# GpSimd ropes q in the second part of a linear attention kernel; one k is summed in PSUM

## The chip, the cores and the metric

The kernel runs on one core of a Trainium2 chip. The metric is the device time of the core in microseconds (us). The core's engines run side by side, each through its own queue in order, and wait for each other on semaphores: TensorE (PE in the profile; PEld is its loading of weights), VectorE (DVE), ScalarE (ACT), GpSimd (POOL) and SyncE (SP), which issues most DMAs. TensorE writes into PSUM, of which there are 8 banks of 128x512 float32 numbers; DVE and ACT read and write PSUM and SBUF; POOL reads and writes SBUF alone.

## The reference

For x of 16 x 1024 rows of 512 numbers:

```python
qkv = x @ Wqkv.T + bqkv
q, k, v = jnp.split(qkv, 3, axis=-1)
q = rmsnorm(q, gq); k = rmsnorm(k, gk)
# 16 heads of 32 numbers
q = apply_rope(q, cos, sin); k = apply_rope(k, cos, sin)
qf = relu(q); kf = relu(k)
vk = einsum('bhlp,bhld->bhpd', [v, 1], kf)
res = einsum('bhpd,bhld->bhlp', vk, qf)
attn = res[..., :-1] / (res[..., -1:] + EPS_LIN)
out = rmsnorm(attn @ Wout.T + bout, gout)
x = layernorm(x + out)
# then a feed-forward layer on x mixed with the row before it
r = sigmoid(xr @ W_r.T); k = square(relu(xk @ W_k.T))
x = layernorm(x + r * (k @ W_v.T))
```

The rope turns pairs of numbers: out_r = t_r cos - t_i sin, out_i = t_r sin + t_i cos. vk is a sum over all 1024 rows of a batch, so q of a batch can be used only when all its k are done.

## The kernel before

Every product in float32 is made of three products of a high and a low half: x = xh + xl and w = wh + wl give xh wh + xh wl + xl wh. ACT makes the high half by a copy that rounds, DVE or POOL the low half by a subtraction. A tile is 128 rows of x; there are 128 tiles, 8 in a batch.

**First part.** It computes q and k of each tile from x's transposed tiles (xt), ropes both, stores q to DRAM (q_d), and adds k into the state of its batch (pskx, four banks; the products of L584, 12 for each tile). The first 8 tiles (SOLO) are done one by one. The other 120 are done as 60 pairs of tiles a and b (`pair`, L1034), which share block products in the manner of Strassen and Winograd: seven products p1 to p7 of six matmuls each (`block_product`, L993) instead of the eight that q and k of two tiles would need. Sums and differences of quarters of xt (s1 to s4, `block_sum`) are made by POOL; their halves, and those of the quarters a1, a2 and a4, by ACT (high, L988) and POOL (low, L990), in `split_block_steps`.

Within a pair, p7 goes to a bank z, which ACT copies into an SBUF tile k2 (`z_out`, L1073). p1 and p2 go to the bank of q of tile a, which ACT has filled with the bias beforehand (`seed`, for the next pair at L1134); between p1 and p2 ACT copies this bank into that of q of b (`y_seed`, L1077). p6 is added to the latter; then DVE writes k of a as this sum and the bias (L1081), adds k2 (L1082), p5 goes to k of a, DVE adds k of a to k2 (`k2_add`, L1085), p4 completes q of b, and p3, in the next pair, k of a. The second half of b_qk holds k's bias less q's (L1270), since the seed carries q's. The next pair begins with p7, then the last pair's p3, then p1, the rest of the last pair's state products, and p2. At the end of a batch the state is turned into m_d, a matrix with the output projection in it (`finish_a`, `finish_b`, `finish_c`).

The rope (`rope_in_steps`, L506) is one squaring on ACT, whose sum goes to rmsnorm, and three operations on DVE: two multiplications by tables (L516 and L518, whose first operand is PSUM except for k of b, which lies in SBUF as k2) and an addition with swapped halves (L521). Its two tables of 256 KB for each q or k are loaded from DRAM by SP (L432), in a ring of five tiles. `rope_k_steps` then makes the reciprocal root on POOL (L148), the halves of relu(k) on ACT (L541, L545) and DVE (L548); POOL adds k to the batch's sum of keys (L556). `split_xn_steps` makes the halves of x for the state (L376 on ACT, L378 on DVE).

From the 29th pair on (WOVEN), output products of the first tiles are interleaved with the pairs.

The order of work around the change is written out by hand as due times: `at(t, fn)` and `steps_at` note that a step is due at t, in units U of one matmul, and all steps are issued in the order of their due times (L1287). PE keeps this order. A scheduler places the instructions of the other engines in their queues by its own model of time.

**Second part** (from L1449, loop at L1533). For each tile j: q of tile j+2 is loaded (`load_q`, L216; three buffers in all), `part_q` (L242) multiplies q of tile j+1 by the sum of keys and scales it on DVE (L246 to L254), `part_qt` transposes it on PE and splits it, `part_m` multiplies it by m_d (psy), `part_y` adds it to x and normalizes (L318, POOL's L148, L327). Between these stand the products of the feed-forward layer (`part_t`, `part_fk`, `part_fr`, `part_fv`) for groups of four tiles. POOL's work here is one low half a tile (mkl, L1335) and the reciprocal roots of L148.

Of the kernel before, what the change touches and what calls it, by code (L numbers as in the profile page):

```python
# [15 lines left out]
P = 128  # L16
# [6 lines left out]
NQ = 1  # L23
# [11 lines left out]
def kernel(  # L35
# [169 lines left out]
    def load_ks(b):  # L205
        ksb[b] = ring("ks", b + (b > 0), 1, 1, [P, DIM], F32, f"ksb{b}")
# [22 lines left out]
    def load_x(j, src=None, early=False):  # L229
        if early:  # L230
            xs[j] = tp.tile([P, DIM], F32, tag="xw", bufs=2, name=f"xw{j}")
        else:
            xs[j] = x_tile(j)
        nc.sync.dma_start(out=xs[j], in_=x[j] if src is None else src)

    def heads(tl):
# [95 lines left out]
    with ExitStack() as a_ctx:  # L332
# [563 lines left out]
        def early(i):  # L896
# [5 lines left out]
            else:  # L902
                tables()
            if i > 1:
                seed(i + 1, 0)
# [46 lines left out]


        def quads():
            for i in range(SOLO, N, 2):
                yield from ((i, 0), (i + 1, 1), (i + 1, 0), (i, 1))

# [22 lines left out]
        def split_block_steps(i, n):  # L980
# [8 lines left out]
            yield  # L989
            G.tensor_sub(t[:, 1], src, f32(t[:, 0]))  # L990

# [42 lines left out]
        def pair(i, t):  # L1034
# [17 lines left out]
            def p1():  # L1052
                block_product(first[a, 0], blk("a1"), lambda w, c: w_q[w][:, c, :])

            def p2():
                block_product(first[a, 0], blk("a2"), lambda w, c: w_q[w][:, 2 + c, :])

# [13 lines left out]
            def z_out():  # L1071
                me["k2"] = rope_tile(b, 1)
                S.copy(me["k2"], me["z"])  # L1073

            def y_seed():
                me["y"] = bank(f"psq{b}")
                S.copy(me["y"], first[a, 0])  # L1077

# [5 lines left out]
            def k2_add():  # L1084
                V.tensor_add(me["k2"], me["k2"], me["a"])  # L1085

            def rope_q_a():
                yield from rope_in_steps(a, 0, first.pop((a, 0)))
                tables()
                load_xn(b)  # L1090

            def rope_k_b():
                yield from rope_in_steps(b, 1, me["k2"], me["k2"])
                tables()

            def rope_q_b():
                yield from rope_in_steps(b, 0, me["y"])
                tables()

            def rope_k_a():  # L1100
                yield from rope_in_steps(a, 1, me["a"])
                tables()

# [27 lines left out]
            tq = tx2 if was is None else max(tx2, t0 + 12 * U + 3.1)  # L1131
            steps_at(rope_q_a(), t + 0.05, tq + 0.45, tq + 1.05, tq + 1.8)
# [6 lines left out]
            steps_at(xn_b, t + 0.45, t + 2.8)  # L1139
            at(t + 2.85, load_xn, a)  # L1140

# [68 lines left out]
            at(t, k2_add)  # L1210
            steps_at(rope_k_b(), t + 0.75, t + 0.8, t + 1.5, t + 2.2)
            at(t, p4)
            t += 6 * U
            steps_at(rope_q_b(), t + 0.05, t + 1.6, t + 2.2, t + 2.95)
            kb = later(rope_k_steps, b)
            steps_at(kb, t + 0.9, t + 1.0, t + 3.2, t + 6.5)
            at(t + 5.2, add_keys, b)
            ts = t + 12 * U
            steps_at(rope_k_a(), ts + 0.05, ts + 1.2, ts + 1.8, ts + 2.5)
            ka = later(rope_k_steps, a)  # L1220
            steps_at(ka, ts + 1.1, ts + 1.15, ts + 4.8, ts + 6.4)
            at(ts + 7.0, add_keys, a)
            xn_a = later(split_xn_steps, a)
            steps_at(xn_a, ts + 2.8, ts + 3.2)
            if r == 2 and j is not None:
                steps_at(later(part_q_steps, j), ty2 + 1.9, ts + 5.9)
            me["p3"], me["rest"] = p3, kx_rest
# [204 lines left out]
        wb = ctx.enter_context(tc.tile_pool(name="workb", reuse_waits="tile", bufs=1))  # L1432
        own["ks"] = wb
        part_fk(0, 0, ps=psk[0])
# [67 lines left out]
    def part_fv(s, t):  # L1502
# [15 lines left out]
        nc.sync.dma_start(out=out[j], in_=xs[j])  # L1518

    ffn = (  # L1520
# [12 lines left out]
    for s in range(NH):  # L1533
        order = ffn if s > 0 else ffn_first
        for u in range(NT):
            j = NT * (s + 2) + u
            if NPRE + NQ < j + 2 < N:
                load_q(j + 2)
            if NPRE + 1 <= j + 1 < N:
                load_x(j + 1)  # L1540
# [10 lines left out]
            if j < N:  # L1551
# [85 lines left out]
```

## Time and profile before

| what | value |
|---|---|
| median of 3 runs | 2866.84 us (2862.26 to 2874.19) |
| the profiled execution | 2863.01 us |
| its span, first to last instruction | 2861.2 us |
| first pair starts / last pair starts (L1073) | 94.6 us / 1320.7 us |
| table loads of 256 KB (L432) | 480, 3.9 us each from issue to landing |
| loads of q (L216) | 128, 2.7 us each |
| largest part of the chain that ended last | PE, 53% of the span |

The profile is that of one execution. Its page gives each engine's busy time, the span in 40 slices, the chain of waits that ended last, and the costliest groups of instructions by line with the mean time of one. Queries of its trace give the same for a stretch of time, the waits, and the timeline. A busy engine is not yet the bound; what counts in a stretch is which engine the others wait for there.

### The profile page before, as it was taken

To read this page: it belongs to the slowest core of one execution; us is meant where nothing else is said; L and a number is where in the kernel's file an instruction comes from. 1 tells how busy PE (TensorE), PEld (TensorE's weight loads), DVE (VectorE), ACT (ScalarE), POOL (GpSimd) and SP (SyncE) were. 2 spreads that over 40 slices of the span, in tenths; PEclk is the share of its full clock that TensorE was granted. 3 is DMA by queue.
4 is the path that set the end of the run, shared out by engine and by line. 5 is a ranking of instruction groups with operands and counts; after the bars stand their busy time and mean duration, and the time that the engine had idled before them with its cause. 6 is when DMAs were issued, how large, how long until landed. Compare 5 with 4: busy or idle time off the path is not lost.

```text
span 2861.2 us, 40565 instructions
## 1 busy us (share of the span) xinstructions
PE 2681.5 (94%) x12212; PEld 2171.1 (76%) x12212; DVE 2420.0 (85%) x4953; ACT 1936.5 (68%) x4068; POOL 1274.5 (45%) x1468
## 2 busy tenths in 40 slices
PE   8888888888988988988999999999999999999999
PEld 6666666666767776766788888888888888888887
DVE  9798788889999999997788888888888887888784
ACT  6556555556565656665687777777777777777876
POOL 6766666667676666674432222222222222222221
PEclk9999999999999999999999999999999999999999
DMA  7676666677877777778333132313232323232211
GB/s 234 199 228 221 213 214 204 206 230 243 260 247 246 232 243 236 236 237 285 122 104 114 56 111 85 115 58 109 88 112 61 106 92 108 65 102 93 91 46 41
DMA packets 240932, 450.08 MB, mean 157 GB/s; under 512 B 25268, under 2 KB 25780, under 8 KB 240712
## 3 DMA queue, kind: packets, MB, share of 16 engines
q1 hardware_dynamic: 240276, 446.83, 48.6%
q8 instruction: 96, 1.57, 0.2%
q14 instruction: 124, 1.02, 0.1%
q10 hardware_dynamic: 436, 0.66, 0.1%
HBM read 329.92 MB, written 117.47 MB: 156 GB/s over the span
## 4 chain that ended last, share of the span: by engine, by line
PE 53%; DVE 1%; DMA 0%; issue 0%; ACT 0%; POOL 0%; POOLq 0%; SPq 0%; DVEq 0%; ACTq 0%
PE psr L188 12%; PE psk L188 12%; PE psv L188 12%; PE psy L188 11%; PE pst L173 2%; PE psqt L173 2%; PE pskx L584 1%; PE psq L997 0%; DMA x<-x_d 0%; DMA w_k<-w_dk 0%; PE psk L997 0%; PE pskv L651 0%; DVE pr L246 0%; DVE t L516 0%; PE psm L700 0%
## 5 line engine op out<-in xcount | busy, mean ns | idle before, releaser
L188 PE MATMUL psk<-mkh,w_k 128*128 128x512 f32 x1024 | 331.9, 395 | 0.1
L188 PE MATMUL psv<-w_v,kah 128*128 128x512 f32 (+1 forms) x1032 | 322.3, 394 | 1.1 <-DVE gate L1514 1.1
L188 PE MATMUL psr<-w_r,mrh 128*128 128x512 f32 x1024 | 318.6, 396 | 0.6 <-DVE halo L1338 0.6
L990 POOL TENSOR_TENSOR blks<-parts,blks 128x256 fp32r<-128x256 f32 x240 | 209.7, 874 | 217.0 <-ACT blks L988 215.6
L188 PE MATMUL psy<-mb,qth 128*128 128x512 f32 x896 | 280.0, 389 | 0.0
L1335 POOL TENSOR_TENSOR mkl<-mixk,mkh 128x512 fp32r<-128x512 f32 x127 | 165.1, 1300 | 194.4 <-ACT mkh L1333 193.4
L556 POOL TENSOR_TENSOR acc<-acc,ro 128x512 f32<-128x512 f32 x112 | 167.2, 1493 | 152.5 <-ACT ro L545 148.9
L997 PE MATMUL psq<-wq_h,blka 128*128 128x512 f32 x480 | 179.8, 415 | 56.7 <-ACT psq L1077 56.7
L188 PEld LDWEIGHTS psk<-mkh,w_k 128*128 128x128 f32 x1024 | 191.3, 188 | 39.0 <-PE pst L173 0.3
L148 POOL TENSOR_TENSOR yrs<-yss,mhalf 128x1 f32<-128x1 f32 x128 | 70.7, 552 | 331.6 <-DVE yss L322 230.7
L188 PEld LDWEIGHTS psv<-w_v,kah 128*128 128x128 f32 x1032 | 188.8, 188 | 38.1 <-DVE gate L1514 1.5
L188 PEld LDWEIGHTS psr<-w_r,mrh 128*128 128x128 f32 x1024 | 188.7, 188 | 37.9 <-ACT r L1376 1.0
L148 POOL TENSOR_TENSOR rsa<-sqa,mhalf 128x1 f32<-128x1 f32 x128 | 79.6, 622 | 304.7 <-DVE sqa L304 293.8
L541 ACT ACTIVATE kh<-ro,rstd_all 128x512 fp32r<-128x512 f32 x128 | 92.7, 725 | 163.0 <-DVE ro L521 110.0
L188 PE MATMUL psv<-w_v,kal 128*128 128x512 f32 (+1 forms) x516 | 200.8, 389 | 0.0
L188 PE MATMUL psk<-mkl,w_k 128*128 128x512 f32 x512 | 199.8, 391 | 0.0
L188 PE MATMUL psr<-w_r,mrl 128*128 128x512 f32 x512 | 196.7, 394 | 0.0
L188 PEld LDWEIGHTS psy<-mb,qth 128*128 128x128 f32 x896 | 168.0, 188 | 34.8
L148 POOL TENSOR_TENSOR rsf<-sqf,mhalf 128x1 f32<-128x1 f32 x128 | 70.2, 555 | 265.6 <-DVE sqf L304 240.4
L584 PE MATMUL pskx<-kl,xnh 128*128 128x512 f32 x512 | 149.7, 400 | 32.7 <-DVE kl L548 32.7
L188 PE MATMUL psy<-mb,qtl 128*128 128x512 f32 x448 | 174.8, 390 | 0.0
L988 ACT CAST blks<-parts 128x256 fp32r<-128x256 f32 x240 | 97.7, 407 | 108.1 <-PE psk L997 67.3
(292 smaller groups left out, 8353.0 us busy)
## 6 DMA issues: line engine op xcount, KB each, us to landing
tab<-tab_d SPq DMA_DIRECT2D x480, 256.0 KB, 3.9
xt<-in_xt_dram SPq DMA_DIRECT2D x128, 256.0 KB, 4.0
xn<-in_x_dram SPq DMA_DIRECT2D x128, 256.0 KB, 3.5
q_d<-ro SPq DMA_DIRECT2D x128, 256.0 KB, 4.0
q<-q_d SPq DMA_DIRECT2D x128, 256.0 KB, 2.7
m_d<-m SPq DMA_DIRECT2D x64, 512.0 KB, 4.3
out_dram<-x SPq DMA_DIRECT2D x127, 256.0 KB, 2.0
x<-in_x_dram SPq DMA_DIRECT2D x120, 256.0 KB, 2.8
```

Of the source, the lines that this page charges most:

```text
L148: G.tensor_tensor(dst, src, mhalf[:, 0 : src.shape[1]], ALU.pow)
L173: T.matmul(ps[:, n * P : (n + 1) * P], lhsT=b, rhs=ident, is_transpose=True, start=(n == 0), stop=(n == NC_ - 1), skip_group_check=True,)
L188: T.matmul(ps, lhsT=a[u][:, rows], rhs=b[w][:, cols], start=(afresh and c == 0 and k == 0), stop=(c == n - 1 and k == 2), skip_group_check ...
L541: S.activation(kh, r, AF.Relu, scale=rstd_all[:, i, 1:2])
L556: G.tensor_add(acc[b], acc[b], r)
L584: T.matmul(ps_kx[b][c], lhsT=a[:, c * P : (c + 1) * P], rhs=r, start=(t == 1 and n == 0), stop=(t == 8 and n == 2),)
L988: S.copy(t[:, 0], src)
L990: G.tensor_sub(t[:, 1], src, f32(t[:, 0]))
L997: T.matmul(ps, lhsT=blk[:, u, c, :], rhs=rhs(w, c), start=(afresh and n == 0), stop=(n == len(order) - 1), skip_group_check=True,)
L1335: (V if by_v else G).tensor_sub(ml, m, f32(mh))
```

## The change

- q of the tiles from 10 on is no longer roped in the first part. DVE adds the bias to it on the way from PSUM to SBUF, ACT squares the result, and it is stored to q_d unroped (`q_out_steps`). In the second part its two tables are loaded (`load_tab`, L1534 of the changed kernel) and POOL ropes it in three operations (`rope_q`, L1539 to L1541), one tile ahead of its use by `part_q`.
- k of tile b is summed into a PSUM bank (`k2_add`), and its rope reads PSUM.
- The banks of q of a are no longer seeded with the bias; p1 starts its bank afresh. b_qk holds the plain bias of k.
- p1 stands ahead of the last pair's p3, `y_seed` after it, then p3, the rest of the state's products, and p2.
- The low halves of a1, a2 and a4 are made by DVE, those of s1 to s4 by POOL as before.
- Due times around these steps are written anew; the ring of tables has four tiles; the sum of keys ksb has one buffer of its own.

```diff
+    def late_q(j):
+        return j >= SOLO + 2
...
-                    tb = wa.tile([P, DIM], F32, tag="tab", bufs=5, name=f"tab{j}{n}{i}")
+                    tb = wa.tile([P, DIM], F32, tag="tab", bufs=4, name=f"tab{j}{n}{i}")
...
+        def q_out_steps(i, ps):
+
+            b_q = b_qk[:, 0:DIM]
+            if not late_q(i):
+                V.tensor_add(ps, ps, b_q)
+                yield
+                yield from rope_in_steps(i, 0, ps)
+                tables()
+                return
+            r = rope_tile(i, 0)
+            V.tensor_add(r, ps, b_q)
+            yield
...
+            S.activation(junk(f"{i}0"), r, AF.Square, accum_out=sums[i][:, 0:1])
+            q_d[i] = dram.tile([P, DIM], F32, name=f"q_d{i}")
+            nc.sync.dma_start(out=q_d[i], in_=r)
...
-            G.tensor_sub(t[:, 1], src, f32(t[:, 0]))
+            (G if n[0] == "s" else V).tensor_sub(t[:, 1], src, f32(t[:, 0]))
...
             def p1():
-                block_product(first[a, 0], blk("a1"), lambda w, c: w_q[w][:, c, :])
+                me["x"] = bank(f"psq{a}")
+                block_product(me["x"], blk("a1"), lambda w, c: w_q[w][:, c, :], afresh=True)
...
             def z_out():
-                me["k2"] = rope_tile(b, 1)
+                me["k2"] = wa.tile([P, DIM], F32, tag="k2", bufs=1, name=f"k2{b}")
...
             def k2_add():
-                V.tensor_add(me["k2"], me["k2"], me["a"])
+                me["k"] = bank(f"psk{b}")
+                V.tensor_add(me["k"], me["k2"], me["a"])
...
             at(t, z_out)
+            at(t, p1)
+            t += 6 * U
+            at(t, y_seed)
             if was is not None:
                 at(t, was["p3"])
                 t += 6 * U
-            ta3 = t
-            at(t, p1)
-            t += 6 * U
-            tx1 = t
-            at(t, y_seed)
-            if was is not None and r != 1:
-                at(t, was["rest"])
-                t += 4 * U
-            tr = t
+                if r != 1:
+                    at(t, was["rest"])
+                    t += 4 * U
             at(t, p2)
...
-            if more:
-                at(tq + 2.6, seed, i + 2, 0)
...
-        V.tensor_sub(b_qk[:, DIM : 2 * DIM], b_qk[:, DIM : 2 * DIM], b_qk[:, 0:DIM])
...
-        at(t, me["p3"])
-        at(t + 6 * U, me["rest"])
+        at(t + 12 * U, me["p3"])
+        at(t + 18 * U, me["rest"])
...
+    def load_tab(j):
+        if late_q(j):
+            tabs[j] = [wb.tile([P, DIM], F32, tag=f"tq{n}", bufs=1, name=f"tq{n}{j}") for n in range(2)]
+            for n in (1, 0):
+                nc.sync.dma_start(out=tabs[j][n], in_=tab_d[j % 8][:, 0, n, :])
+
+    def rope_q(j):
+        if late_q(j):
+            q, (c, t) = qs[j], tabs.pop(j)
+            G.tensor_mul(t, q, t)
+            G.tensor_mul(c, q, c)
+            G.tensor_add(halves(q), halves(c), halves(t)[:, :, ::-1, :])
...
                 load_q(j + 2)
+                load_tab(j + 2)
...
                     part_y(j, ps)
+                if NPRE + NQ < j + 2 < N:
+                    rope_q(j + 2)
```

More of the change, by code (lines that the diff above doesn't have):

```diff
@@ L205, in load_ks @@
     def load_ks(b):
-        ksb[b] = ring("ks", b + (b > 0), 1, 1, [P, DIM], F32, f"ksb{b}")
+        ksb[b] = tp.tile([P, DIM], F32, tag="ks", bufs=1, name=f"ksb{b}")
         nc.sync.dma_start(
@@ L903, in early @@
                 tables()
-            if i > 1:
+            if 1 < i < SOLO - 1:
                 seed(i + 1, 0)
@@ L951, in late_step @@
                     late_load(i)
+        def q_out_steps(i, ps):
[9 more added lines that the diff above has]
+            yield
+            if i not in sums:
+                sums[i] = wa.tile([P, 2], F32, tag="ss", bufs=3, name=f"ss{i}")
+            S.activation(junk(f"{i}0"), r, AF.Square, accum_out=sums[i][:, 0:1])
+            q_d[i] = dram.tile([P, DIM], F32, name=f"q_d{i}")
+            nc.sync.dma_start(out=q_d[i], in_=r)
         def quads():
             for i in range(SOLO, N, 2):
-                yield from ((i, 0), (i + 1, 1), (i + 1, 0), (i, 1))
+                yield from (n for n in ((i, 0), (i + 1, 1), (i + 1, 0), (i, 1)) if n[1] or not late_q(i))
         quad = quads()
@@ L1052, in p1 @@
             def p1():
-                block_product(first[a, 0], blk("a1"), lambda w, c: w_q[w][:, c, :])
+                me["x"] = bank(f"psq{a}")
+                block_product(me["x"], blk("a1"), lambda w, c: w_q[w][:, c, :], afresh=True)
             def p2():
-                block_product(first[a, 0], blk("a2"), lambda w, c: w_q[w][:, 2 + c, :])
+                block_product(me["x"], blk("a2"), lambda w, c: w_q[w][:, 2 + c, :])
             def p6():
@@ L1076, in y_seed @@
                 me["y"] = bank(f"psq{b}")
-                S.copy(me["y"], first[a, 0])
+                S.copy(me["y"], me["x"])
             def a_seed():
@@ L1084, in k2_add, with rope_of @@
             def k2_add():
-                V.tensor_add(me["k2"], me["k2"], me["a"])
-            def rope_q_a():
-                yield from rope_in_steps(a, 0, first.pop((a, 0)))
+                me["k"] = bank(f"psk{b}")
+                V.tensor_add(me["k"], me["k2"], me["a"])
+            def rope_of(n, j, ps):
+                yield from rope_in_steps(n, j, ps())
                 tables()
[L1090 to L1102, printed above, removed]
+            q_a = later(lambda: q_out_steps(a, me["x"]))
+            q_b = later(lambda: q_out_steps(b, me["y"]))
+            rope_k_b = rope_of(b, 1, lambda: me["k"])
+            rope_k_a = rope_of(a, 1, lambda: me["a"])
             kx_one = later(add_kx_steps, one, (8,))
@@ L1130, in pair @@
             tx2 = t
-            tq = tx2 if was is None else max(tx2, t0 + 12 * U + 3.1)
-            steps_at(rope_q_a(), t + 0.05, tq + 0.45, tq + 1.05, tq + 1.8)
-            if more:
-                at(tq + 2.6, seed, i + 2, 0)
+            steps_at(q_a, *(t + d for d in ((0.05, 0.75) if late_q(a) else (0.0, 0.05, 0.45, 1.05, 1.8))))
+            at(max(t - 0.3, t0 + 5.8), load_xn, b)
             at(t, next, kx_one)
@@ L1138, in pair @@
             xn_b = later(split_xn_steps, b)
-            steps_at(xn_b, t + 0.45, t + 2.8)
-            at(t + 2.85, load_xn, a)
+            steps_at(xn_b, t + 1.2, t + 1.4)
+            at(t + 1.45, load_xn, a)
             if r == 0 and j is not None and 0 < j <= NPRE:
@@ L1210, in pair @@
             at(t, k2_add)
-            steps_at(rope_k_b(), t + 0.75, t + 0.8, t + 1.5, t + 2.2)
+            steps_at(rope_k_b, t + 0.7, t + 0.72, t + 2.06, t + 2.8)
             at(t, p4)
             t += 6 * U
-            steps_at(rope_q_b(), t + 0.05, t + 1.6, t + 2.2, t + 2.95)
+            steps_at(q_b, *(t + d for d in ((0.03, 0.75) if late_q(b) else (0.0, 0.03, 1.5, 2.1, 2.8))))
             kb = later(rope_k_steps, b)
[L1216 to L1219, printed above, removed]
+            steps_at(kb, t + 1.4, t + 1.45, t + 2.2, t + 3.6)
+            at(t + 3.6, add_keys, b)
+            ts = t + 18 * U
+            steps_at(rope_k_a, ts + 0.05, ts + 0.1, ts + 0.8, ts + 1.5)
             ka = later(rope_k_steps, a)
-            steps_at(ka, ts + 1.1, ts + 1.15, ts + 4.8, ts + 6.4)
-            at(ts + 7.0, add_keys, a)
+            steps_at(ka, ts + 0.75, ts + 0.8, ts + 2.3, ts + 3.6)
+            at(ts + 3.7, add_keys, a)
             xn_a = later(split_xn_steps, a)
-            steps_at(xn_a, ts + 2.8, ts + 3.2)
+            steps_at(xn_a, t + 5.05, t + 5.7)
             if r == 2 and j is not None:
-                steps_at(later(part_q_steps, j), ty2 + 1.9, ts + 5.9)
+                steps_at(later(part_q_steps, j), ty2 + 1.9, t + 8.6)
             me["p3"], me["rest"] = p3, kx_rest
@@ L1432 @@
         wb = ctx.enter_context(tc.tile_pool(name="workb", reuse_waits="tile", bufs=1))
-        own["ks"] = wb
         part_fk(0, 0, ps=psk[0])
@@ L1518, in part_fv @@
         nc.sync.dma_start(out=out[j], in_=xs[j])
+    tabs = {}
+    def load_tab(j):
[9 more added lines that the diff above has]
+            G.tensor_add(halves(q), halves(c), halves(t)[:, :, ::-1, :])
     ffn = (
```

## The prediction

> **What bounds the kernel now.** I read the page first, its busy line and the rows of the slices.
>
> ```profile
> PE 2681.5 (94%) x12212; PEld 2171.1 (76%) x12212; DVE 2420.0 (85%) x4953; ACT 1936.5 (68%) x4068; POOL 1274.5 (45%) x1468
> ...
> PE   8888888888988988988999999999999999999999
> ...
> DVE  9798788889999999997788888888888887888784
> ...
> POOL 6766666667676666674432222222222222222221
> ```
>
> The reader is to see two programs in one. Up to slice 18 (about 1340 us) PE has holes, DVE is nearly full and POOL two thirds busy. After it PE is full, DVE has a little room and POOL looks idle. The busy shares over the whole span hide this, so the second view is the busy time by stretch. Its columns are the stretch, its length, then PE, PEld, DVE, ACT and POOL with their instructions, the granted clock, the DMA share and GB/s. The first row is the 28 pairs before block products are interleaved with the output of other tiles, the second the 32 pairs with it (bounds from the start times of L1073, one per pair, 94.6 to 1320.7); the last lies in the second part.
>
> ```profile
> 94.60:687.60 593.00, 509.17 (x2160) 399.26 (x2161) 515.78 (x734) 336.56 (x769) 382.92 (x416) 0.96 0.69 219
> 687.60:1340.70 653.10, 586.61 (x2614) 462.80 (x2613) 613.65 (x943) 399.47 (x917) 431.93 (x478) 1.00 0.76 241
> 1600.00:2600.00 1000.00, 1000.00 (x4740) 829.93 (x4739) 824.29 (x2164) 762.55 (x1523) 250.97 (x338) 1.00 0.29 92
> ```
>
> In the 32 pairs DVE is busy 613.65 of 653.10 us (94%): DVE is the bound. In the 28 it is 87%, with the clock at 0.96. In the second part PE is busy for all of the 1000 us; a tile takes 11.8 us there (85 of them by the count of L327), of which DVE is busy 824.29/85 = 9.7.
>
> PE's own need in a pair: the chain's pieces of 36 equal matmuls last 8.21 us, 0.228 us each. A pair has 7 products of 6 and 24 for the state, 66 in all, 15.0 us. Four pairs add the finish and, in the 32, one output product and transposes: some 6.8 us without and 9.5 us with them, from 0.228 us each and the 32 small matmuls of L651 and L659. So PE needs 7 x (60.2 + 6.8) = 469 us in the first stretch and 8 x (60.2 + 9.5) = 558 us in the second.
>
> Third, the groups of DVE in four such pairs (769.1 to 850.2 us); after the bar are the busy us and the mean ns of one:
>
> ```profile
> L548 DVE TENSOR_TENSOR kl<-ro,kh 128x512 fp32r<-128x512 f32 x7 | 9.1, 1301 | 0.3
> L378 DVE TENSOR_TENSOR xnl<-xn,xnh 128x512 fp32r<-128x512 f32 x8 | 9.0, 1131 | 0.5 <-ACT xnh L376 0.5
> L521 DVE TENSOR_TENSOR ro<-psq,t 128x512 f32<-128x512 f32 x8 | 5.5, 690 | 0.2
> L516 DVE TENSOR_TENSOR t<-psq,tab 128x512 f32<-128x512 f32 x8 | 5.5, 686 | 0.4
> L518 DVE TENSOR_TENSOR psq<-psq,tab 128x512 f32<-128x512 f32 x8 | 5.5, 686 | 0.0
> L516 DVE TENSOR_TENSOR t<-ro,tab 128x512 f32<-128x512 f32 x4 | 4.1, 1022 | 0.1
> L685 DVE TENSOR_TENSOR kvtl<-kv,kvth 128x256 fp32r<-128x256 f32 x2 | 1.4, 697 | 0.5 <-ACT kvth L683 0.5
> ```
>
> An operation of one size costs about 685 ns when one input is in PSUM and 1022 to 1301 ns when both are in SBUF. POOL works beside them, on SBUF alone. The timeline of the second part shows what happens:
>
> ```profile
> 2003.01 1.28 POOL L1335 TENSOR_TENSOR mkl<-mixk,mkh 128x512 fp32r<-128x512 f32 x1
> 2003.08 1.23 DVE L308 TENSOR_TENSOR nma<-nma,rsa 128x1 f32<-128x1 f32 x1 [0.73 <-POOL rsa L148]
> 2004.23 0.74 DVE L1319 SCALAR_TENSOR_TENSOR mixr<-pst,omm_r,mixr 128x511 f32<-128x511 f32 x1
> ```
>
> One number per partition took 1.23 us, until POOL's operation ended. So POOL's work is not free for DVE. Its price, from the groups of 1600 to 2600 us:
>
> ```profile
> L327 DVE SCALAR_TENSOR_TENSOR x<-y,yrs,x 128x512 f32<-128x512 f32 x85 | 82.3, 968 | 14.1 <-POOL yrs L148 13.9 <-issue 0.2
> L1323 DVE SCALAR_TENSOR_TENSOR mixr<-halo,omm_r,mixr 128x1 f32<-128x1 f32 x41 | 36.4, 887 | 0.0
> L253 DVE TENSOR_SCALAR den<-den,rstd_all 128x16 f32<-128x16 f32 x85 | 28.6, 336 | 1.6
> L308 DVE TENSOR_TENSOR nma<-nma,rsa 128x1 f32<-128x1 f32 x85 | 25.3, 298 | 50.0 <-POOL rsa L148 50.0
> ```
>
> Undisturbed these take 752 (median of L327), 209 (the same operation for mixk), 226 (L251) and 150 ns (nmf). The excess is 85 x 0.216 + 41 x 0.678 + 85 x 0.110 + 85 x 0.148 = 68 us, or 0.80 us for each of the 85 mkl of L1335, which last 1.29 us.
>
> **First part, DVE, for four pairs.** Removed: q's rope, 24 operations, 16.5 us. Added: 8 additions of the bias from PSUM at 0.685, 5.5 us. The second tile's k rope now reads PSUM: 4 x (1.022 + 0.984 + 0.898) becomes 4 x 3 x 0.683, which saves 3.4 us. The low halves of a1, a2 and a4 come over from POOL: 12 operations of 128x256 in SBUF; L685 is the same shape, 0.41 to 0.97 us, so 4.9 to 11.6; I take its mean here, 0.697, 8.4 us. POOL loses these 12 (about 0.86 each, 10.3 of its 55 us per four pairs), and the excess that kl, xnl and ss suffer (4.3 + 3.6 + 1.8 us over 681, 680 and 155 ns) should fall by that fifth: 1.8 us. Sum: -11.0 - 3.4 + 8.4 - 1.8 = -7.8 us.
>
> DVE's need becomes 515.8 - 7 x 7.8 = 461 and 613.7 - 8 x 7.8 = 551 us, as much as PE's 469 and 558. Two even engines in static order wait for each other. Today the stretches last 1.15 and 1.06 times the larger need; I take 1.10 for both: 516 and 614 us, gains of 77 and 39, **116 us** together. The bounds are 1.15 for both (65 us) and 1.064 for both (153 us).
>
> What else changes there is counted at nothing, being off DVE. The seed's copy goes (0.58 us on ACT per pair, and ACT is 61% busy). p1 moves ahead of p3, so that the copy of x (L1077, now 27 us of PE waits in 29 pairs) lies beside p3 and the state's products; if PE is the bound that is up to 0.9 us a pair, inside the 153. A pair needs five banks of four, but in the built order each is drained by work that stands well before its next user; a wait of 0.7 us a pair (one eviction) is inside the 65. Of the 480 table loads 236 leave SP's queue here, which no DVE wait above names. The last pair's p3 gets a due time 12 units (2.7 us) later, with no work put ahead of it: at most that.
>
> **Second part, for 118 tiles.** POOL gets two multiplications and one addition of 128x512 in SBUF. No row shows the addition over swapped halves; L437 has runs of 16 too and takes 1.29 to 1.82 us, so 3.9 to 5.5 us a tile beside POOL's 3.0 of 11.8: there is room. SP gets two loads of 256 KB a tile. They wait for the rope before them, and behind them stand the store of out and the loads of x and q. By the page's 446.83 MB at 48.6% they add some 13 points to a DMA share of 29%, and q is used a tile later, so I cost them at nothing.
>
> DVE pays. Three operations at 0.80 us of stall each are 2.4 us, so 9.7 + 2.4 = 12.1 us against PE's 11.8: DVE becomes the bound, by 0.3 us with no slack and 0.7 at 3%. I take 0.4 us, **47 us** in all. Bounds: in the first part's pairs the same excess with that of k's three SBUF operations is (9.7 + 3.4 us)/55 of POOL's busy time, 0.24, which would be 0.9 us a tile and leave DVE at 10.6: nothing lost. A stall of the full 1.29 us gives 13.6, 1.8 us a tile, 212 us. I stay with 0.80, the row of the same stage and size.
>
> The wait added there: in the built order the rope's first two operations stand ahead of L148's yrs, for which L327 waits on DVE, and everything behind L327. q lands 2.7 us after its issue at 2007.4, two operations later it is 2012.7, and yrs is done at 2013.2 where it was 2010.1. The new order puts mixr, den and q's scaling (some 2.1 us, and the stalls themselves) ahead of L327, which covers it. Without that cover it is 1 us a tile.
>
> The Trainium skill, "GPSIMD Engine Reference", sections "Key points" and "Engine selection", speaks against this half of the change: GpSimd shares its SBUF interfaces with VectorE, which collide when DVE reads two SBUF inputs or runs in a two-port mode, and element by element work belongs on VectorE. The trace agrees (0.80 us above). By that rule alone six large operations a tile are exposed (pr, q, x twice, mrl, kal), and the sum would lean to the upper bound. The same skill's "TensorE: Matmul & The Clock Gate", section "HAM oscillation", says that idle gaps put the clock to half; the 0.96 of the first 28 pairs agrees, and by it fuller PE work would return some of that.
>
> **The sum.** The profiled execution took 2863.0 us for a span of 2861.2, and the median of the runs is 2866.84, 0.13% more. 2863 - 116 + 47 = **2794 us**.
>
> **The rivals.**
> - POOL's ropes fall into DVE's 2.1 idle us and PE stays full in the second part. For it: the 0.24 of the first part; against: 0.80 per mkl. 2863 - 116 = 2747 us. Chance 0.28.
> - The first part gains its least, since waits between two even engines take the place of the load: 2863 - 65 + 47 = 2845 us. For it: 1.15 in the 28 pairs today, where DVE is only 87% busy. Chance 0.14.
> - Slower: POOL's ropes bound the second part through DVE. Two ropes in a row find DVE at its one-column operations, each held to the end. At 1.2 us each a tile takes 9.7 + 3.6 = 13.3 us, 1.5 more, 177 us: 2924 us. It decides from about 1.0 us of stall each, where the loss of 1.0 us a tile eats the 116. For it: the 1.23 us above; against: 3.5 of DVE's 9.7 us there read PSUM (y, qtl, mixk, mixr, gate) and are not held. Chance 0.16.
>
> The forecast has 0.42, and reaches from 2760 to 2830. The range of 2725 to 2875 takes in the first two rivals, the first with a gain of up to 138 us; beyond it are the slower rival's most and a little below, under 0.2. A measurement can tell some 0.5% from no change, 14 us. Faster: 0.42 + 0.28 + half of 0.14, less a little of the forecast's edge, 0.75; within it 0.10; slower 0.15, the third rival less its low edge.
>
> **What would show it.** Right: the stretch of pairs shorter by 116 us with DVE still above 90%; kl and xnl a little under 1301 and 1131; k's t from PSUM at 685; a tile in the second part near 12.2 us with DVE above 95% and PE below 100; x, pr, q, kal or mrl above 800 ns beside the ropes. Wrong: 11.8 us a tile (first rival); above 12.8 (third); pairs still above 20 us; or PE waits on banks, y's copy or the low halves named in the pairs.

## The result and the profile after

The changed kernel takes 2979.83 us (median of 4 runs, 2976.38 to 2983.45), the kernel before 2864.55 us beside it (4 runs, 2860.73 to 2874.19): a ratio of 1.0397, with a 95% interval of 1.0367 to 1.0427. It is 4% slower; 2794 us was forecast. The profiled execution took 2978.49 us for a span of 2976.7.

The two halves of the forecast part company. The page of the kernel after, its busy line and three rows of the 40 slices:

```profile
PE 2712.2 (91%) x12212; PEld 2169.9 (73%) x12212; DVE 2439.7 (82%) x4898; ACT 1915.3 (64%) x4008; POOL 1591.5 (53%) x1642
...
PE   8899999999999999889988988988988988988999
...
DVE  8888888888888888778888888888788888788884
...
POOL 6555555555555555465555555555555555555541
```

PE's row has changed sides: at nine tenths or more from the third to the sixteenth slice, where it had holes, and with holes behind them, where it was full. The stretches put times to it (columns as in the prediction; the pairs are cut at the start of `z_out`, the first, the 29th and the last pair):

```profile
92.70:614.00 521.30, 483.71 (x2165) 387.61 (x2164) 431.88 (x716) 320.73 (x740) 290.64 (x331) 0.99 0.60 196
614.00:1198.20 584.20, 557.92 (x2533) 451.73 (x2532) 480.74 (x882) 376.30 (x864) 331.09 (x378) 1.00 0.64 206
1600.00:2600.00 1000.00, 888.58 (x4043) 705.43 (x4042) 836.96 (x1837) 653.53 (x1296) 525.46 (x505) 0.99 0.37 116
```

From the first pair's start to the last pair's it is 1105.5 us, where it was 1226.1: **120.6 us gained**. From the first x of the second part (L330, L327 before) to the last it is 1659.8 us, where it was 1417.7: **242.1 us lost**. What lies around them changed by 6 us. The time of a tile is taken below from 96 tiles in the middle of the second part: 11.80 us before, **13.91** after. In the last row DVE is busy 837 us and PE 889, so no engine is full: 72 tiles have 11.6 us of DVE each, and 2.3 us in which it waits.

The chain that ended last could be followed back only to 2635 us, over the last 12% of the span, so it says nothing of the pairs or of most of the second part. Within that piece PE has less than half of it:

```profile
PE 5%; DVE 3%; DMA 1%; issue 1%; ACT 1%; POOL 1%; SPq 0%; POOLq 0%; ACTq 0%
```

What holds DVE is seen in the timeline of the second part after:

```profile
2105.72 0.69 DVE L321 TENSOR_TENSOR y<-psy,g_out 128x512 f32<-128x512 f32 x1
2106.28 1.29 POOL L1539 TENSOR_TENSOR tq<-q,tq 128x512 f32<-128x512 f32 x1 [0.56 <-DMA q<-q_d]
2106.32 1.79 DVE L249 SCALAR_TENSOR_TENSOR pr<-q,ksb 128x512 f32<-128x512 f32 x1
2107.52 1.74 POOL L1540 TENSOR_TENSOR tq<-q,tq 128x512 f32<-128x512 f32 x1
2108.04 1.78 DVE L1344 TENSOR_TENSOR mrl<-mixr,mrh 128x512 fp32r<-128x512 f32 x1
```

y, which reads PSUM, takes its 0.69 us. pr and mrl, with both inputs in SBUF, take 1.79 and 1.78 beside the rope's multiplications, where they took 0.68 and 0.69 before; and POOL's second multiplication takes 1.74, where its median is 1.30. Each holds the other: pr ends 0.54 us after the first multiplication, the second multiplication 1.15 us after pr, and mrl 0.56 us after that, about as if each did its work only when the other had ended. Over 1000 us the groups of DVE are (busy, mean ns | waits before), first those of pr and mrl in the kernel before:

```profile
L1335 DVE TENSOR_TENSOR mrl<-mixr,mrh 128x512 fp32r<-128x512 f32 x85 | 58.3, 686 | 14.9 <-ACT mrh L1333 14.9
L246 DVE SCALAR_TENSOR_TENSOR pr<-q,ksb 128x512 f32<-128x512 f32 x85 | 57.9, 681 | 0.0
```

and after:

```profile
L330 DVE SCALAR_TENSOR_TENSOR x<-y,yrs,x 128x512 f32<-128x512 f32 x73 | 85.7, 1174 | 72.6 <-POOL yrs L148 72.6
L1344 DVE TENSOR_TENSOR mrl<-mixr,mrh 128x512 fp32r<-128x512 f32 x72 | 75.2, 1044 | 1.2 <-ACT mrh L1342 1.2
L1386 DVE TENSOR_TENSOR kal<-r,kah 128x512 fp32r<-128x512 f32 x72 | 68.1, 946 | 24.7 <-ACT r L1385 24.1
L249 DVE SCALAR_TENSOR_TENSOR pr<-q,ksb 128x512 f32<-128x512 f32 x72 | 58.3, 809 | 0.0
L321 DVE TENSOR_TENSOR y<-psy,g_out 128x512 f32<-128x512 f32 x72 | 48.9, 679 | 0.0
```

x was 968 ns with 13.9 us of waits for yrs; it is 1174, and the waits are 72.6 us for fewer tiles. y, which reads PSUM, stays at 679. A third thing shows only in the waits of SP's own queue:

```profile
SPq L1534 <- POOL q L1541: 328.1, 54, 11.3
```

For 328 of 1000 us SP stands at a table load (L1534) until POOL has done the rope of the tile before, whose tables lie in the only buffers; the next q's load stands behind it.

### The profile page after: what moved, and what is told of

Same layout as the page of the kernel before. It is cut to its first block, busy times and chain, and to the rows that moved or that the text cites. A ratio compares the mean times of both kernels' runs of the same rounds, so it can differ in the third digit from the quotient of the medians.

```text
span 2976.7 us, 40561 instructions
## 1 busy us (share of the span) xinstructions
PE 2712.2 (91%) x12212; PEld 2169.9 (73%) x12212; DVE 2439.7 (82%) x4898; ACT 1915.3 (64%) x4008; POOL 1591.5 (53%) x1642
## 5 line engine op out<-in xcount | busy, mean ns | idle before, releaser
L188 PE MATMUL psr<-w_r,mrh 128*128 128x512 f32 x1024 | 344.7, 418 | 72.5 <-ACT junky L323 36.4
L188 PE MATMUL psv<-w_v,kah 128*128 128x512 f32 (+1 forms) x1032 | 329.1, 401 | 23.2 <-ACT junky L323 23.2
L1011 POOL TENSOR_TENSOR blks<-parts,blks 128x256 fp32r<-128x256 f32 x240 | 189.0, 787 | 195.8 <-ACT blks L1009 195.5
L1539 POOL TENSOR_TENSOR tq<-q,tq 128x512 f32<-128x512 f32 x118 | 163.1, 1383 | 181.8 <-DMA q<-q_d 119.3
L305 ACT ACTIVATE junka<-x,nma 128x512 bf16<-128x512 f32 x120 | 86.7, 722 | 238.7 <-DVE nma L303 238.3
L330 DVE SCALAR_TENSOR_TENSOR x<-y,yrs,x 128x512 f32<-128x512 f32 x120 | 140.2, 1169 | 111.3 <-POOL yrs L148 111.3
L1344 POOL TENSOR_TENSOR mkl<-mixk,mkh 128x512 fp32r<-128x512 f32 x127 | 172.3, 1357 | 105.2 <-ACT mkh L1342 99.9
L188 PE MATMUL psr<-w_r,mrl 128*128 128x512 f32 x512 | 205.3, 407 | 0.0
L1018 PE MATMUL psq<-wq_h,blka 128*128 128x512 f32 x480 | 170.8, 397 | 21.8 <-DVE ro L967 13.8
```

What stands on the lines that cost most here:

```text
L188: T.matmul(ps, lhsT=a[u][:, rows], rhs=b[w][:, cols], start=(afresh and c == 0 and k == 0), stop=(c == n - 1 and k == 2), skip_group_check ...
L305: S.activation(junk(name), xt, AF.Square, bias=nm, accum_out=sq)
L330: V.scalar_tensor_tensor(xs[j], y, rs, xs[j], ALU.mult, ALU.add, accum_out=sm)
L1011: (G if n[0] == "s" else V).tensor_sub(t[:, 1], src, f32(t[:, 0]))
L1018: T.matmul(ps, lhsT=blk[:, u, c, :], rhs=rhs(w, c), start=(afresh and n == 0), stop=(n == len(order) - 1), skip_group_check=True,)
L1344: (V if by_v else G).tensor_sub(ml, m, f32(mh))
```

## The experiments

Each is the changed kernel with one edit. Of each the time of one execution is given, with the kernel before at 2861 to 2869 us beside it, unless more is said. The theories were: POOL's in-order queue (the roots that DVE waits for stand behind the rope); the hold (POOL's large operations and DVE's on SBUF delay each other); the loads (SP's queue, one buffer for each table).

**e1_rope_in_first_part**: q roped by DVE in the pairs again; the other edits stay.

```diff
     def late_q(j):
-        return j >= SOLO + 2
+        return False
```

> q is roped by DVE in the first part for every tile, all other edits of the change stay. All theories expect the second part back at 11.8 us a tile. For the first part, the prediction's own prices say that DVE has, against before, 5.5 us more for four pairs from the bias, 8.4 more from the low halves and 3.4 + 1.8 less from k and POOL: some 8.7 us in all for four pairs, so pairs 130 us longer than before and 2990 us. If the order of the products and the banks were what shortened the pairs, it would be 2860 or less.

2825.89 us, and a tile in the second part 11.80 us as before. So the whole loss comes from q's late rope, and the other edits gain 39 us in the pairs (1187.1 us), where the forecast's prices gave 130 us more. No run tells apart which of them (the order of the products, the banks, the seeds, the due times) gains it. The pairs' stretches:

```profile
94.70:657.40 562.70, 496.29 (x2163) 385.55 (x2162) 529.11 (x875) 322.32 (x740) 285.69 (x331) 0.99 0.72 231
657.40:1281.80 624.40, 569.36 (x2533) 451.54 (x2532) 587.32 (x1068) 373.61 (x864) 317.03 (x379) 0.99 0.76 245
```

DVE is busy for 94% of both: it is the fullest engine there as long as it ropes q. Taking the rope away gives the other 82 us and leaves PE as the fullest (558 of 584 us).

**e2_no_rope**: the three POOL operations left out, the loads kept.

> The second part's three operations on POOL are left out, so q stays unroped there; the loads of q and of both tables stay. Theories A (POOL's queue: the rope holds back the reciprocal root of y, and DVE stands at x) and B (port: DVE is held while POOL works on SBUF) both expect 11.8 us a tile and 2740 us. Theory C (the added loads keep SP's queue and delay q and x) expects a tile above 13 us and more than 2880 us.

2863.78 us, as none of the theories had it. From the 24th tile on a tile takes 11.8 us: the loads by themselves cost nothing there. In the first 24 a tile takes up to 18.4 us (mean of eight). PE waits there for loads of m_d (43.8 us in the whole run) and DVE for x. Why they come late is not settled, so for the start of the second part this run does not clear the loads.

**e3_rope_behind_roots**: the rope's operations forced, in POOL's queue, behind the roots of the tile before.

```diff
+            last = last_of(mybir.EngineType.Pool)
+            for op, args in (
...
+                op(*args)
+                not_before(last_of(mybir.EngineType.Pool), last)
```

> As the change, but POOL's three rope operations are put behind both reciprocal roots of part_y (yrs, rsa) of the tile before in POOL's queue, and nothing else. Theory A expects that DVE's wait for yrs (1.0 us a tile) goes and the tile falls to 12.3 us or less: 2800 us. Theory B expects that DVE's held operations stay, 1.9 us a tile, and that the tile stays at 13.4 us or above: 2930 us or more.

3075.05 us, 14.63 us a tile: worse. DVE's x waits only 20.8 us for yrs in 1000 us, yet the tile is longer; PE now waits 96.5 us at the transposes of q. So x's wait for yrs is not what sets the tile. But the edit also makes the rope itself late, so it does not clear POOL's queue as a cause.

**e4_rope_on_dve**: the three operations on DVE instead of POOL, in the second part.

```diff
-            G.tensor_mul(t, q, t)
+            V.tensor_mul(t, q, t)
...
```

> As the change, but DVE does the three rope operations of the second part. DVE gets 3 x 0.685 = 2.05 us a tile and POOL's queue is as before. Theory B: DVE's need is 9.7 + 2.05 = 11.8 us, even with PE, 12.0 to 12.5 us a tile, 2770 to 2820 us, faster than the change although DVE does the work. Theory A, in its pure form (only DVE's stand at yrs counts): also about 12 us. If DVE's in-order queue is what is tight whatever the reason, the rope's wait for the load of q now stands in DVE's own queue, and it is above 13 us, 2880 us or more.

2825.66 us, 12.48 us a tile. DVE, given three operations more, takes 11.3 us a tile, and the tile is 1.4 us shorter than with POOL's help. DVE waits 44 us for the tables' loads.

**e5_small_ops_in_queue**: six small POOL operations in the rope's place.

```diff
-            G.tensor_mul(t, q, t)
-            G.tensor_mul(c, q, c)
-            G.tensor_add(halves(q), halves(c), halves(t)[:, :, ::-1, :])
+            for two in (q, t, c, c, q, q):
+                rsqrt(two[:, 0:2], rstd_all[:, j, :])
```

> Leaves q's rope out for the tiles of the second part: its three POOL operations of 128x512 become six of POOL's small ones (128x2, the form of yrs and rsa, about 0.6 us each), at the same place in POOL's queue, behind the same waits (q and both tables landed). POOL is held as long as by the rope (some 3.7 us a tile), but reads and writes almost nothing. If what costs is POOL's queue (the roots yrs, rsa and rsf come late, whatever stands ahead of them), a tile stays at 13.3 to 13.9 us, and DVE's x still waits over 50 us for yrs in 1000 us. If what costs is that POOL's large operations hold DVE's, a tile goes to 11.8 to 12.2 us, and x, mrl, kal and pr go back to 968, 690, 690 and 690 ns. In between, the share is read from the time of a tile.

2902.22 us, in two regimes: 14.7 us a tile up to the 48th, 12.06 from the 56th on. In the first, POOL waits for the tables (67.7 of 300 us) and SP for POOL (104.6); in the second neither wait is among the larger ones. That pointed to a loop through SP's queue, and this run could not price queue and hold.

**e7_half_late_dve** and **e7b_half_late_pool**: one tile of each pair has its late rope, by DVE or by POOL.

```diff
     def late_q(j):
-        return j >= SOLO + 2
+        return j >= SOLO + 2 and j % 2 == 0
...
-                yield from (n for n in ((i, 0), (i + 1, 1), (i + 1, 0), (i, 1)) if n[1] or not late_q(i))
+                yield from (n for n in ((i, 0), (i + 1, 1), (i + 1, 0), (i, 1)) if n[1] or not late_q(n[0]))
...
```

> Only one tile of each pair has its rope in the second part, by DVE; the other's stays in the pairs. By the sums so far the pairs give 39 us without the move and 121 with all of it, so about 80 with half. If DVE's added 1.0 us a tile lies in its slack (9.7 of 11.8 us), a tile stays at 11.8 us and the time is 2863 - 80 = 2783 us. If every operation added to DVE there lengthens the tile in proportion (12.5 us with all ropes on DVE, so 0.35 with half), the second part loses 41 us and the time is about 2825.

> The same half, but by POOL as in the changed kernel. If the loss is in proportion to the POOL operations, a tile takes 12.85 us on the mean and the time is 2783 + 122 = 2905 us. If there is a slack that the first operations use up, a tile takes under 12.4 us and the time is under 2850.

2827.84 and 2911.64 us. On DVE the half costs 0.05 us a tile (11.85, PE busy for 999.7 of 1000 us), on POOL 0.79 (12.59): 0.53 us for each POOL operation against 0.70 with all, so there is no slack that the first operations use up. The pairs gain only 46 us (1179.7 us), 7 more than without any late rope, and not half of 82; DVE is at 85% and PE at 90% there. Why is not settled: the due times are written for both tiles of a pair alike, and no others were tried.

**e8_low_halves_on_pool**: the low halves of a1, a2 and a4 back on POOL.

```diff
-            (G if n[0] == "s" else V).tensor_sub(t[:, 1], src, f32(t[:, 0]))
+            G.tensor_sub(t[:, 1], src, f32(t[:, 0]))
```

> The changed kernel with the low halves of a1, a2 and a4 back on POOL. It tests the term of 8.4 us on DVE for four pairs (12 x 0.519 = 6.2 by the run). If DVE sets the time of the pairs, the pairs' stretch falls from 1105 us by 15 times some 4 us (6.2 less what POOL's 12 operations more hold DVE, about 1.8), to about 1045, and DVE is below 90%. If PE and DVE are even there, or POOL's block halves come late and PE waits for them, the stretch stays within 20 us of 1105 or is longer. The second part is the changed kernel's, 13.9 us a tile.

2976.56 us, and the pairs the same to 1.2 us:

```profile
95.70:620.80 525.10, 491.43 (x2162) 397.01 (x2161) 405.18 (x631) 321.00 (x741) 358.57 (x416) 0.97 0.61 194
620.80:1202.40 581.60, 555.50 (x2534) 452.52 (x2533) 446.51 (x789) 376.81 (x865) 402.69 (x472) 1.00 0.65 207
```

DVE is busy 61 us less than after and the time is the same. In the changed kernel DVE is not the bound of the pairs, and where these halves are made is worth nothing there.

**e11_tables_ahead**: two buffers for each table, loaded a tile further ahead and behind q's load in SP's queue; the k activations' halves have four buffers instead of five to make room.

```diff
-            kh = wb.tile([P, HT], F32R, tag="kah", bufs=5, name=f"kah{s}{o}")
+            kh = wb.tile([P, HT], F32R, tag="kah", bufs=4, name=f"kah{s}{o}")
...
-            tabs[j] = [wb.tile([P, DIM], F32, tag=f"tq{n}", bufs=1, name=f"tq{n}{j}") for n in range(2)]
+            behind = last_of(mybir.EngineType.SP)
+            tabs[j] = [wb.tile([P, DIM], F32, tag=f"tq{n}", bufs=2, name=f"tq{n}{j}") for n in range(2)]
             for n in (1, 0):
                 nc.sync.dma_start(out=tabs[j][n], in_=tab_d[j % 8][:, 0, n, :])
+                not_before(last_of(mybir.EngineType.SP), behind)
...
-                load_tab(j + 2)
+                if not tabs:
+                    load_tab(j + 2)
+                load_tab(j + 3)
```

> The loop theory: in the changed kernel the loads of the two tables have one buffer each, so in SP's queue they wait for the rope of the tile before (SP waited 328.1 us for POOL's q in 1000 us); q's next load is queued behind them and lands 3 to 6 us later; POOL's first multiplication waits for it; yrs and mkl stand behind that on POOL, and the rope's addition behind those, which releases the next loads. One turn of that loop is the tile. Here the tables have two buffers each and are loaded one tile further ahead, behind q's load in SP's queue, so that nothing on SP waits for the rope just before. To make room, the high and low halves of the k activations have four buffers instead of five, which can only cost. The rope stays on POOL, with the same three operations. Loop theory: a tile goes from 13.9 to at most 12.4 us, the time to 2770 to 2800 us, and SP's wait for POOL's q falls below 60 us. Port theory (POOL's operations hold DVE's): a tile stays at 13.3 us or more, the time above 2905 us.

2927.93 us, 13.40 us a tile. SP's wait for the rope is gone:

```profile
SPq L1535 <- POOL q L1543: 3.0, 8, 0.6
```

and only 0.5 of the 2.1 us with it. The loop costs something but is not the main cause; that theory falls as the whole answer.

**e12_tables_ahead_dve**: the same loads, the rope on DVE as in e4.

> The same loads ahead, but the rope's three operations on DVE. If the 12.5 us a tile of the rope on DVE with single buffers came from waits for the loads, DVE's need of 11.3 us fits under PE's 11.8: a tile takes 11.8 to 12.1 us and the time is 2745 to 2780 us. If DVE at 90% cannot be fed in this order anyway, a tile stays at 12.4 us or more, about 2820 us.

2787.74 us, 12.08 us a tile: faster than both kernels. DVE is busy for 11.2 us a tile. In e11 it is busy for 11.4, nearly the same, and the tile takes 13.40: DVE's busy time does not tell the tile's length.

**e14_tables_ahead_behind_roots**: the order of e3 with the loads of e11.

> Loads ahead, the rope on POOL, and each of its operations behind the roots of the tile before in POOL's queue (the order that gave 14.65 us a tile with single buffers). Loop theory: the longer loop was what made it slow, so with the loop open a tile takes at most 12.4 us here too, and DVE's x waits under 25 us for yrs in 1000 us. If that order is bad in itself (the rope late for pr and the transposes of q), a tile stays above 13.3 us.

3068.32 us, 14.65 us a tile. Of the loop theory's two signs one came, x waits 19.9 us for yrs, and the tile did not. But in this order the loop is not open: SP stands at the tables' loads for the rope again,

```profile
SPq L1535 <- POOL q L1547: 187.6, 56, 7.2
```

where e11 has 3.0 us. So whether the order is bad in itself is not shown. The granted clock is 0.94 in 1600 to 2600 us, as in e3.

**e15_small_ops_tables_ahead** (e5's edit on e11), **e16_no_roots_on_pool** (on e11) and **e17_one_of_three_on_pool** (on e11) part queue and hold. e5's edit is above; e17 puts the multiplication by the cosines on POOL and the other two operations on DVE; e16's is:

```diff
     def rsqrt(dst, src):
-        G.tensor_tensor(dst, src, mhalf[:, 0 : src.shape[1]], ALU.pow)
+        if second:
+            V.tensor_scalar(dst, src, 1.0, 0.0, ALU.mult, ALU.add)
+        else:
+            G.tensor_tensor(dst, src, mhalf[:, 0 : src.shape[1]], ALU.pow)
```

> Leaves q's rope out for the tiles of the second part: six of POOL's small operations (128x2, some 0.6 us each) in its place, as before, but with the tables loaded one tile ahead, so that the loop through SP's queue is open. POOL is held as long as by the rope, with the same waits on q, and moves almost no data. If the 13.4 us a tile with the loads ahead and the rope on POOL comes from POOL's queue (roots late), a tile takes at least 13.0 us here. If it comes from DVE's operations being held by POOL's large ones, a tile takes 11.8 to 12.1 us from the first tiles on, without the 14.7 us of the single buffers.

> The counterpart: the rope's three large operations stay on POOL, loads ahead, but in the second part yrs, rsa and rsf are no roots: DVE writes them with one operation of 128x1 (a multiplication by one, so the output is another). Nothing that DVE or ACT waits for stands behind the rope in POOL's queue, but mkl. DVE gets three small operations a tile more, 0.15 us each if not held. Queue theory: a tile falls from 13.4 to at most 12.3 us. Port theory: it stays at 12.9 us or more. Both, if the two together: between, and the sum of what the two experiments save is more than the 1.6 us that the rope costs.

> Loads ahead; the multiplication by the cosines on POOL, the other two operations of the rope on DVE. With all three on DVE a tile takes 12.08 us, with all three on POOL 13.40. If each POOL operation costs the same, 12.5 us; if POOL's first one is free (it has 54% of its time idle, and DVE is given 0.68 us back), 11.8 to 12.0 us and a time under 2775 us; if the hand-over between the engines costs more than the operation, above 12.7 us.

2777.57, 2858.85 and 2834.55 us; a tile takes 12.04, 12.76 and 12.60 us. The two stretches below are e11's and e15's:

```profile
1600.00:2600.00 1000.00, 914.88 (x4184) 725.00 (x4184) 853.68 (x1918) 671.00 (x1348) 542.03 (x526) 1.00 0.37 119
```

```profile
1600.00:2600.00 1000.00, 992.66 (x4674) 816.15 (x4673) 808.65 (x2129) 748.31 (x1506) 632.00 (x837) 1.00 0.42 134
```

In e15 POOL is busy longer than in e11 (632 against 542 us), with the same waits and in the same place, and PE is nearly full. What went is the large operations' reading and writing of SBUF. DVE's operations show it, in e11 first:

```profile
L330 DVE SCALAR_TENSOR_TENSOR x<-y,yrs,x 128x512 f32<-128x512 f32 x75 | 91.6, 1221 | 47.8 <-POOL yrs L148 47.8
L257 DVE SCALAR_TENSOR_TENSOR q<-q,den 128x512 f32<-128x512 f32 x75 | 73.9, 986 | 1.6
```

and in e15:

```profile
L330 DVE SCALAR_TENSOR_TENSOR x<-y,yrs,x 128x512 f32<-128x512 f32 x83 | 82.4, 992 | 84.5 <-POOL yrs L148 82.0 <-DMA out_dram<-x 2.5
L257 DVE SCALAR_TENSOR_TENSOR q<-q,den 128x512 f32<-128x512 f32 x83 | 57.3, 691 | 2.5
```

DVE waits longer for yrs in e15 (82.0 us) than in e11 (47.8), and the tile is 1.36 us shorter: a wait that the trace names need not be what costs. In e16 the roots are out of the queue and the large operations stay: 0.65 us better than e11, with 0.44 us a tile more on DVE. With the 1.36 of e15 that is 2.01 us, more than the 1.6 that the rope costs: the sign named above for queue and hold acting together. In e17 one large operation on POOL costs 0.52 us more than on DVE, and the three of e11 1.32, so 0.44 each: in proportion, with POOL busy below 40%.

**e18_rope_on_dve_ahead_timed**: e12 again, timed.

> The version with the rope on DVE and the tables loaded a tile ahead, timed against the kernel before: 2788 us by one look, so a ratio of 0.973 to 0.976, which keeps 75 of the 120 us that the pairs give. If the one look was lucky, above 0.98.

2787.67 us (median of 4, 2783.19 to 2789.93), a ratio of 0.9725 to before, interval 0.9701 to 0.9750: 2.7% faster. In its second part:

```profile
1600.00:2600.00 1000.00, 986.90 (x4647) 810.67 (x4647) 929.05 (x2370) 752.60 (x1498) 274.29 (x333) 1.00 0.43 134
```

DVE is busy for 93%, more than in any kernel with POOL's help, and PE for 99%.

## Why the prediction was wrong

**The first part** was right in sum: 120.6 us for a forecast of 116, split 71.7 and 48.9 where 77 and 39 were given (to the last pair's start). Its terms were not. DVE's need fell from 76.7 to 62.3 us in four pairs, by 14.5 where 7.8 was forecast. The groups of DVE in those four pairs (690.6 to 765.8 us) after:

```profile
L551 DVE TENSOR_TENSOR kl<-ro,kh 128x512 fp32r<-128x512 f32 x7 | 7.6, 1081 | 2.1 <-ACT ro L548 2.1
L1011 DVE TENSOR_TENSOR blka<-xt,blka 128x256 fp32r<-128x256 f32 x12 | 6.2, 519 | 1.0 <-ACT blka L1009 1.0
L381 DVE TENSOR_TENSOR xnl<-xn,xnh 128x512 fp32r<-128x512 f32 x8 | 5.7, 717 | 2.7 <-ACT xnh L379 2.7
L519 DVE TENSOR_TENSOR t<-psk,tab 128x512 f32<-128x512 f32 x8 | 5.5, 686 | 3.1 <-ACT junk L513 3.1
```

The low halves cost 6.2 us instead of 8.4. The excess of kl, xnl and ss fell by 5.8 us (1.5, 3.3 and 1.0), not 1.8. The twelve operations that POOL lost explain little of that: e8 gives them back, and DVE's other work in the pairs rises by 29 us (the 90.3 us of these halves leave it, its busy time falls by 60.9), 2.0 us for four pairs. The rest comes with the other edits. k's t from PSUM takes 686 ns, as said. So DVE came to 83 and 82%, not above 90, and PE, with 95% in the second stretch, is the fullest engine. The forecast also asked PE's need, times 1.10; PE's stretches were 1.08 and 1.05 times its busy time.

That the sum held was in part luck. By the forecast's terms q's rope is 16.5 us of DVE's work for four pairs, and all other edits add 8.7. In e1, where only the others act, DVE's busy time in the pairs rose by 6 us, not 130, and the pairs were 39 us shorter, 30 of them in the first 28 pairs, where DVE went from 87 to 94% busy. What the forecast priced as a loss or "counted at nothing" thus gave a third of the gain, and the rope the other two. The granted clock of the first 28 pairs rose too, from 0.96 to 0.99, and PE's busy time there fell by 25 us; the forecast leaned to that with its last citation but did not price it.

**The second part** failed: +47 us forecast, +242 measured. The term of the hold itself was near: 0.80 us for each POOL operation was taken, DVE's busy time rose from 9.7 to 11.6 us a tile, 0.64 each. POOL's durations too: 1.39, 1.46 and 1.45 us, 4.3 in sum, within 3.9 to 5.5. The step that failed is the one behind it: "9.7 + 2.4 = 12.1 us against PE's 11.8: DVE becomes the bound, by 0.3 us with no slack". It added the holds to DVE's busy time and took the tile as the larger of two sums, so that DVE's 2.1 idle us a tile would swallow most of them. For work of DVE's own that room is there: in e12 the rope itself fills it, DVE is busy for 11.2 us a tile, and the tile takes 12.08. For holds it is not: in e11 DVE is busy for 11.4 us and idle for 2.0, and the tile takes 13.40. The price of POOL's large operations, against small ones that keep POOL as long, is 1.36 us a tile (13.40 in e11, 12.04 in e15). How they lengthen the tile is argued, not shown: x waits for yrs, nma for rsa, mrl for ACT's mrh, each with the next tile's work in order behind it, and a hold that falls on that path would lengthen the tile though DVE is not full. Even the upper bound, 1.29 us of stall for each operation and 13.6 us a tile, was too low, since it too was a sum of DVE's busy time.

That the loads of the tables were cost "at nothing" failed as well: 0.51 us a tile (13.91 to 13.40, at least, since e11 has fewer buffers elsewhere), though not by bandwidth, which the forecast had looked at, but by the wait on SP's queue for the rope. The forecast had named that wait, and what stands behind it, and priced neither.

The wait for yrs was taken as covered, and as 1 us a tile without the cover: with the loads ahead, the queue without large operations costs 0.24 us (12.04 in e15 against 11.80), so the cover was nearly enough. With the large operations present, taking the roots out returns 0.65 (e16). These do not add up with 1.36 in a unique way; how much of the 1.36 acts through late roots stays open.

Step by step, from before to e15, e11 and after, 0.24 us for the queue, 1.36 for the large operations and 0.51 for the loads make the 2.11 us a tile; other steps would part it otherwise. The third rival had the right side, DVE held by POOL's rope, and its 13.3 us a tile was nearest. That was luck in the number: it took 1.2 us for each hold, where DVE's busy time shows 0.64, and DVE as the bound, which at 84% it is not. The first two rivals fell: the ropes were not hidden, and the pairs gained what the forecast gave, not their least.

The Trainium skill's "GPSIMD Engine Reference" says in section "Key points" that GpSimd contends with VectorE for SBUF where DVE reads two SBUF inputs; pr at 1.79 us beside POOL's multiplication, and y from PSUM, at 0.68 on the mean as before, agree. Its section "Engine selection" puts element by element work of two inputs on VectorE as about twice as fast; here 1.29 us against 0.69 for the operation itself, and 13.40 against 12.08 us for the tile.

## What to carry to other kernels

Idle time of an engine in an in-order pipeline has no single price. Here VectorE's 2.1 idle us a tile took the rope as VectorE's own work for 0.28 us, while holds by GpSimd that made VectorE about as busy cost 1.6: look whether the added work, or what it delays, lies on the path between engines, and do not price by the busy times alone. Work moved to an idle engine that holds the other's operations may cost more than leaving it on a busy one; time it on both. A load with one buffer makes its queue wait for the last user, and everything behind it in that queue waits too (here SP for 328 of 1000 us, some 0.5 us a tile).

## What the runs showed of the hardware

- POOL's operation is held as well as DVE's: the rope's second multiplication takes 1.30 us by its median and 1.74 beside pr and mrl, which take 1.79 and 1.78 for 0.69. y, with one input in PSUM, takes 0.68 on the mean before and after.
- The granted clock was lowest where PE's holes were long. From 1600 to 2600 us PE stands still 17 times for 5.6 to 7.1 us in e3, and the clock is 0.94; in the kernel after no hole is over 2.2 us, and it is 0.99; in e11 none is over 1.9, and it is 1.00. In the first 28 pairs before, with holes of up to 3.3 us, the clock stood at half in 13 short stretches, 51 us in all, hence the 0.96. Whether the length or the sum of the holes counts, these runs do not tell.
- e5 shows two lasting regimes of one program, 14.7 and 12.06 us a tile. In the slow one POOL and SP wait for each other; what makes it pass over into the other is not shown. With two buffers (e15) the slow one does not last.
